# The sixteen routing values of a row block: from the row tile to small tiles loaded five blocks ahead

## The chip, the cores and the metric

The kernel runs on one core of a Trainium2 chip. A core has five engines with instruction queues of their own: TensorE (PE, matmuls), VectorE (DVE), ScalarE (ACT), GpSimd (POOL) and SyncE (SP, here only a DMA queue). The metric is the time of one execution on the device, in microseconds (us); lower is better. A profile of one execution tells what each engine did and what it waited for.

## The reference

Eight sequences of 512 tokens, width 256, float32, go through a state-space layer, a mixture of experts, causal attention and the same mixture again, each with a layer norm ahead and a residual sum. The change lies in the mixture:

```python
combine = (jax.nn.one_hot(topk_idx, E, dtype=tw.dtype) * tw[..., None]).sum(1)
h = jnp.einsum('td,edf->etf', x, gate_w)
u = jnp.einsum('td,edf->etf', x, up_w)
y = jnp.einsum('etf,efd->etd', jax.nn.silu(h) * u, down_w)
routed = jnp.einsum('etd,te->td', y, combine)
```

There are 16 experts with hidden width 256, and each of the 4096 tokens takes its best 4. The kernel computes only these: tokens are sorted by expert, and each expert's tokens are worked on in blocks of 128.

## The kernel before

The kernel has four stages: the scan with the router of the first mixture, the routed experts of the first mixture (`routed(0, ...)`), attention with the router of the second, and the routed experts again (`routed(1, ...)`). The routers write each token's normalised row once for each chosen expert into a DRAM tensor `xg`, sorted by expert. A row of `xg` has 256 values and then 16 routing values: four gains, four expert numbers and eight copies of the token's number.

`routed` works through 136 blocks (a branch for more, `needed > LIKELY`, is not taken with these inputs). For block n:

- `load(n)`, four blocks ahead (`AHEAD`): four DMAs on SP (L874) bring the 256 values of 128 rows, and one DMA on ScalarE (L878) brings the 16 routing values into the same row tile (tag `kb4`, nine buffers). The first two blocks come with one DMA each (L870). The address of a block in `xg` is a register; for every eight blocks `places` loads eight addresses from SBUF on SP and on ScalarE (L848).
- `fetch(n)`: ScalarE and VectorE copy the expert's gate and up weights (L893) into small tiles (tag `col`, six buffers, so three blocks); the expert's place is a register too, loaded for four blocks at a time on TensorE, ScalarE and VectorE (L834).
- `turn(n)`: VectorE transposes the rows (L906).
- `up(n)`: TensorE multiplies (L919, eight matmuls for gate and eight for up as the profile counts them); ScalarE takes the sigmoid (L927); VectorE multiplies twice (L929, L930) and computes each row's gain from the routing values (L934, L942). The PSUM results have two buffers each.
- `down(n)`: TensorE multiplies by the down weights (L949), ScalarE scales by the gain (L957), and GpSimd scatters the rows, adding to a DRAM tensor `parts` (L958), with the token numbers from the routing values as index. Even and odd blocks go to two `parts` tensors.

In program order, iteration n of `run` has `load(n + 4)`, `fetch(n + 1)`, `up(n)`, `turn(n + 2)` and `down(n - 2)`. The framework then orders each engine's instructions by its own plan of times, under dependences; `tc.issue_after(x)` puts an instruction behind x on its engine. Each engine works through its queue in that order. DMAs take completion semaphores in turn, eight for those of SP and ScalarE and eight for GpSimd's, and one is issued only when the last DMA on its semaphore has landed. A tile's buffer is free for a new load when everything that used it is done; for a row tile the scatter is last.

At the start of the kernel, three constants `bp_sb`, `cp_sb` and `bc_all` (L178 to L250) have tiles of their own; `bc_sb` is made from them on VectorE (L198, the line of the helper `by_vector`).

Of the kernel before, what the change touches and what calls it, by code (L numbers as in the profile page):

```python
# [10 lines left out]
FP = mybir.dt.float32  # L11
AF = mybir.ActivationFunctionType
# [19 lines left out]
EG, TKG, TK = 4, 2, 4  # L32
# [3 lines left out]
BLK = P  # L36
# [8 lines left out]
ROW = D + 2 * TK + 8  # L45
# [8 lines left out]
U32 = mybir.dt.uint32  # L54
EPS = 1e-5
CLIP = 10.0
KB, COLS = 9, 6
# [2 lines left out]
SENT = 4  # L60
HELD = 6
AHEAD = 4


SUMMED = {0: DONE[0], 1: 76, 2: 88, 3: 110, 4: 127}
# [12 lines left out]
def tile_hybrid_block(  # L78
# [22 lines left out]
    nc = tc.nc  # L101

    const = ctx.enter_context(tc.tile_pool(name="const", bufs=1))
    xpool = ctx.enter_context(tc.tile_pool(name="xpool", bufs=3))
    work = ctx.enter_context(tc.tile_pool(name="work", bufs=2))
    small = ctx.enter_context(tc.tile_pool(name="small", bufs=2))
# [18 lines left out]
    xg = [dram.tile([NROW, ROW], FP, name=f"xg_{i}") for i in range(2)]  # L125
# [49 lines left out]
    nc.gpsimd.dma_start(out=b_in_sb, in_=b_in.rearrange("(c p) -> p c", p=P))  # L175
    d_sb = const.tile([P, NI], FP, name="d_sb")
    nc.gpsimd.dma_start(out=d_sb, in_=d_skip.rearrange("(c p) -> p c", p=P))
    bp_sb = const.tile([P, NI, DS], FP, name="bp_sb")  # L178
    nc.gpsimd.dma_start(out=bp_sb, in_=b_proj.rearrange("(c p) j -> p c j", p=P))
    cp_sb = const.tile([P, NI, DS], FP, name="cp_sb")  # L180
    nc.gpsimd.dma_start(out=cp_sb, in_=c_proj_t.rearrange("(c p) j -> p c j", p=P))
    w_out_sb = w_scan[:, KD * DI :].rearrange("p (c d) -> p c d", c=NI)
    nc.scalar.dma_start(out=w_out_sb, in_=w_out.rearrange("(c p) d -> p c d", p=P))
# [13 lines left out]
    def by_vector(op, *args):  # L197
        pending.append(lambda: tc.keep_in_program_order(op(*args)))  # L198
# [18 lines left out]
    def load_expert(e: int):  # L217
# [13 lines left out]
        out=before,  # L231
        in_=before,
# [12 lines left out]
    nc.scalar.activation(begun, decay, AF.Sigmoid)  # L245


    bc_all = const.tile([P, NI, DS], FP, name="bc_all")
    by_vector(nc.vector.tensor_mul, bc_all, bp_sb, cp_sb)
    bc_sb = const.tile([P, NI], FP, name="bc_sb")  # L250
    by_vector(nc.vector.tensor_reduce, bc_sb, bc_all, AX.X, ALU.add)
# [1 line left out]
    def load_attention_weights():  # L253
# [16 lines left out]
        out=causal, in_=causal, compare_op=ALU.is_ge, fill=0.0, base=0, pattern=[[0, 2], [1, P]], channel_multiplier=-1  # L270
# [6 lines left out]
        out=tri, in_=tri, compare_op=ALU.is_gt, fill=0.0, base=0, pattern=[[1, P]], channel_multiplier=-1  # L277
# [546 lines left out]
    def routed(i: int, table, beside):  # L824

        weight_at, row_at, expert, many, _ = table
        ACT, DVE = mybir.EngineType.Activation, mybir.EngineType.DVE
        PE, SP = mybir.EngineType.PE, mybir.EngineType.SP
        held, heads, known, turns = {}, set(), set(), {}

        def values(n: int):

            many = min(4, (LIKELY if n < LIKELY else NBLK) - n)
            _, w = nc.values_load_multi_w_load_instructions(  # L834
                weight_at[:, n : n + many],
                engines=[PE, ACT, DVE],
                min_val=0,
                max_val=(E - 1) * WEXP,
                skip_runtime_bounds_check_because="a count of at most E - 1 experts, times WEXP",
            )  # L840
            for j in range(many):
                held[n + j].insert(0, w[j])
                known.add(n + j)

        def places(n: int):

            many = min(8, (LIKELY if n < LIKELY else NBLK) - n)
            _, r = nc.values_load_multi_w_load_instructions(  # L848
                row_at[:, n : n + many],
                engines=[SP, ACT],  # L850
                min_val=0,
                max_val=NROW - BLK,
                skip_runtime_bounds_check_because="the blocks table stays within the sorted rows",
            )
            for j in range(many):
                held[n + j] = [r[j]]

        def load(n: int):
            if n not in held:
                places(n)  # L860
            if n < 2:


                rows = work.tile([P, NT, ROW], FP, tag="rows", name=f"rows_{i}_{n}")
                rows = rows.rearrange("p t c -> p (t c)")[:, 0 : 4 * D]
            else:
                rows = work.tile([P, 4 * D], FP, tag="kb4", name=f"rows_{i}_{n}", bufs=KB)
            block = bass.ds(held[n][-1], BLK)
            if n in heads:
                nc.sync.dma_start(out=rows[:, 0:ROW], in_=xg[i][block, :])  # L870
            else:

                for a in range(QUAD):
                    nc.sync.dma_start(  # L874
                        out=rows[a * SQ : (a + 1) * SQ, 0:D].rearrange("s (b c) -> s b c", b=QUAD),
                        in_=xg[i][block, a * KD * SQ : (a + 1) * KD * SQ].rearrange("(b s) c -> s b c", s=SQ),
                    )
                nc.scalar.dma_start(out=rows[:, D:ROW], in_=xg[i][block, D:ROW])  # L878
            held[n].append(rows)

        def fetch(n: int):
# [29 lines left out]
        def up(n: int):  # L911
            _, _, rows, *both = held[n]


            ph = [bank([P, KF * P], f"ph_{i}_{n}_{s}", f"big{s}") for s in range(2)]
            for s in range(2):
                for f in range(KF):
                    for k in range(KD):
                        nc.tensor.matmul(  # L919
                            ph[s][:, f * P : (f + 1) * P],  # L920
                            lhsT=both[s][:, k * F + f * P : k * F + (f + 1) * P],
                            rhs=rows[:, ROW + k * P : ROW + (k + 1) * P],
                            start=(k == 0),
                            stop=(k == KD - 1),
                        )
            act = rows[:, ROW + D : ROW + D + F]
            nc.scalar.activation(act, ph[0], AF.Sigmoid)  # L927
            with tc.issue_after(turns.pop(n + 1).ins) if n + 1 in turns else nullcontext():
                nc.vector.tensor_mul(act, ph[0], act)  # L929
            made = nc.vector.tensor_mul(act, ph[1], act)  # L930

            gain = small.tile([P, TK + 1], FP, tag="gain", name=f"gain_{i}_{n}", bufs=4)
            with tc.issue_after(made.ins):
                nc.vector.scalar_tensor_tensor(  # L934
                    gain[:, 0:TK],
                    rows[:, D + TK : D + 2 * TK],
                    expert[:, n : n + 1],
                    rows[:, D : D + TK],
                    ALU.is_equal,
                    ALU.mult,  # L940
                )
            nc.vector.tensor_reduce(gain[:, TK : TK + 1], gain[:, 0:TK], AX.X, ALU.add)  # L942
            held[n][3:] = [act, gain]

        def down(n: int):
            w, _, rows, act, gain = held.pop(n)
            py = bank([P, D], f"pyr_{i}_{n}", "y")
            for f in range(KF):
                nc.tensor.matmul(  # L949
                    py,  # L950
                    lhsT=act[:, f * P : (f + 1) * P],
                    rhs=w_all[:, bass.ds(w + 2 * KD * F + f * D, D)],
                    start=(f == 0),
                    stop=(f == KF - 1),
                )

            nc.scalar.mul(rows[:, 0:D], py, gain[:, TK : TK + 1])  # L957
            nc.gpsimd.indirect_dma_start(  # L958
                out=parts[i][n % 2],
                out_offset=bass.IndirectOffsetOnAxis(  # L960
                    ap=rows[:, D + 2 * TK : D + 2 * TK + 1].bitcast(U32), axis=0
                ),
                in_=rows[:, 0:D],
                in_offset=None,
                compute_op=ALU.add,
            )

        def run(first: int, last: int):
            heads.update((first, first + 1))
            coming = iter(range(first, last))  # L970

            def load_to(n: int):
                for m in coming:
                    load(m)
                    if m >= n:
                        break

            load_to(first + AHEAD - 1)
            values(first)
            fetch(first)  # L980
            turn(first)
            for n in range(first, last + 2):
                load_to(n + AHEAD)
                if n + 2 < last and n + 2 not in known:
                    values(n + 2)
                if n + 1 < last:
                    fetch(n + 1)
                if n < last:
# [598 lines left out]
```

## Time and profile before

| | |
|---|---|
| median of three runs | 1736.51 us (1733.36 to 1739.04) |
| profiled execution | 1726.62 us |
| its span, first to last instruction | 1724.9 us |
| mean granted TensorE clock | 0.978 |
| TensorE busy | 1596.2 us (93%) |
| VectorE, ScalarE, GpSimd busy | 1183.2, 717.7, 773.3 us |
| scatters L958 | 272, 1570 ns each on GpSimd |
| address loads L848 on ScalarE | 34, median 1968 ns |
| 16-value loads L878 on ScalarE | 268, median 343 ns to issue |

An engine's busy time is the union of its instructions; DMA issues, register loads and semaphore waits are not counted as busy. A line of the timeline has the start, the duration, the engine (with a q for its sequencer), the source line, the operation, output and inputs, and in brackets how long the engine was idle before and what ended that. [...]

### The profile page before, as it was taken

To read this page: it belongs to the slowest core of one execution; us is meant where nothing else is said; L and a number is where in the kernel's file an instruction comes from. 1 tells how busy PE (TensorE), PEld (TensorE's weight loads), DVE (VectorE), ACT (ScalarE), POOL (GpSimd) and SP (SyncE) were. 2 spreads that over 40 slices of the span, in tenths; PEclk is the share of its full clock that TensorE was granted. 3 is DMA by queue.
4 is the path that set the end of the run, shared out by engine and by line. 5 is a ranking of instruction groups with operands and counts; after the bars stand their busy time and mean duration, and the time that the engine had idled before them with its cause. 6 is when DMAs were issued, how large, how long until landed. Compare 5 with 4: busy or idle time off the path is not lost. (4 is left out here: it accounts for less than half of the span.)

```text
span 1724.9 us, 35522 instructions
## 1 busy us (share of the span) xinstructions
PE 1596.2 (93%) x9912; PEld 1150.6 (67%) x9912; DVE 1183.2 (69%) x3771; ACT 717.7 (42%) x1416; POOL 773.3 (45%) x675
## 2 busy tenths in 40 slices
PE   6899998989999999899999999999899999888884
PEld 3566655589998888854445545544458999888883
DVE  7888877546666666567786686776745866656553
ACT  3223232145554444455544354344214455444441
POOL 3355555535555555430032232232433555555453
PEclk8999999999999999999999999999998999999997
DMA  4454333457776666631012211122545677667667
GB/s 161 143 179 157 136 107 115 161 84 101 101 102 115 93 94 93 100 78 38 25 59 75 70 59 63 58 84 86 183 136 81 98 101 106 115 123 134 104 111 182
DMA packets 297530, 181.63 MB, mean 105 GB/s; under 512 B 204816, under 2 KB 278064, under 8 KB 297328
## 3 DMA queue, kind: packets, MB, share of 16 engines
q0 software_dynamic: 54720, 82.57, 24.9%
q1 hardware_dynamic: 202208, 90.57, 20.6%
q10 hardware_dynamic: 40400, 6.15, 2.1%
q8 instruction: 84, 1.38, 0.3%
q14 instruction: 118, 0.97, 0.2%
HBM read 81.62 MB, written 97.53 MB: 104 GB/s over the span
## 5 line engine op out<-in xcount | busy, mean ns | idle before, releaser
L958 POOL DMA_INDIRECT part<-rows x272 | 427.0, 1570 | 341.2 <-DMA rows<-xg 198.1
L724 POOL DMA_INDIRECT xg<-sorted_m,slots_m x256 | 259.7, 1014 | 322.0 <-ACT slots_m L721 81.6
L919 PE MATMUL ph<-rows,gate 128*128 128x128 f32 x2160 | 291.2, 278 | 43.4 <-DVE rows L906 41.9
L919 PEld LDWEIGHTS ph<-rows,gate 128*128 128x128 f32 x2160 | 279.6, 193 | 75.9 <-issue 44.7
L919 PE MATMUL ph<-rows,up 128*128 128x128 f32 x2160 | 288.1, 277 | 0.0
L949 PE MATMUL pyr<-w_all,rows 128*128 x1088 | 281.9, 383 | 2.9 <-DVE gain L934 2.7
L919 PEld LDWEIGHTS ph<-rows,up 128*128 128x128 f32 x2160 | 265.6, 194 | 0.0
L893 DVE COPY up<-w_all 128x512 f32 x270 | 118.6, 439 | 152.1 <-PE ph L919 125.8
L893 ACT COPY gate<-w_all 128x512 f32 x270 | 166.0, 617 | 125.5 <-PE ph L919 90.9
L949 PEld LDWEIGHTS pyr<-w_all,rows 128*128 128x128 f32 x1088 | 187.7, 193 | 19.3 <-ACT rows L927 3.1
L927 ACT ACTIVATE rows<-ph 128x256 f32<-128x256 f32 x272 | 104.2, 383 | 201.1 <-PE ph L919 169.0
L906 DVE STREAM_TRANSPOSE rows<-rows 128x256 f32<-128x256 f32 x268 | 117.7, 439 | 80.6 <-DMA rows<-xg 72.9
L957 ACT ACTIVATE rows<-pyr,gain 128x256 f32<-128x256 f32 x272 | 128.5, 473 | 87.4 <-PE pyr L949 60.2
L1171 ACT ACTIVATE w_all<-ps_a 128x1024 f32<-128x1024 f32 x128 | 124.4, 1020 | 52.2 <-PE ps_a L1160 47.8
L929 DVE TENSOR_TENSOR rows<-ph,rows 128x256 f32<-128x256 f32 x272 | 106.8, 393 | 46.5 <-ACT rows L927 45.5
L930 DVE TENSOR_TENSOR rows<-ph,rows 128x256 f32<-128x256 f32 x272 | 115.0, 423 | 25.4 <-PE ph L919 1.1
L1160 PE MATMUL ps_a<-w_all 32*128 32x384 f32 (+3 forms) x1024 | 122.2, 475 | 7.7 <-ACT w_all L1171 6.7
L1022 PE MATMUL pg_m<-xT_m,su_sb 128*128 128x512 f32 x256 | 124.8, 609 | 0.0
L1022 PE MATMUL pg_m<-xT_m,sg_sb 128*128 128x512 f32 x256 | 122.4, 600 | 0.0
L1051 PE MATMUL pd_m<-sd_sb,act_m 128*128 128x256 f32 x512 | 121.2, 383 | 0.3 <-DVE act_m L1038 0.2
L1051 PEld LDWEIGHTS pd_m<-sd_sb,act_m 128*128 128x128 f32 x512 | 95.9, 190 | 24.0 <-issue 6.7
L1160 PEld LDWEIGHTS ps_a<-w_all 32*128 32x128 f32 x1024 | 48.4, 186 | 69.4 <-ACT w_all L1171 25.7
(224 smaller groups left out, 1979.7 us busy)
## 6 DMA issues: line engine op xcount, KB each, us to landing
rows<-xg SPq DMA_DIRECT2D x1072, 32.0 KB
part<-x SPq DMA_DIRECT2D x16, 512.0 KB
part<-ys_m SPq DMA_DIRECT2D x14, 512.0 KB
w_all<-in_L_ffn_gate_w_dram SPq DMA_DIRECT2D x24, 256.0 KB
w_all<-in_L_ffn_up_w_dram SPq DMA_DIRECT2D x24, 256.0 KB
w_all<-in_L_ffn_down_w_dram SPq DMA_DIRECT2D x24, 256.0 KB
sum<-part POOLq DMA_DIRECT2D x10, 512.0 KB
xg<-zeros SPq DMA_DIRECT2D x34, 136.0 KB
```

The lines of the kernel that those rows point to most:

```text
L724: nc.gpsimd.indirect_dma_start(out=xg[i], out_offset=bass.IndirectOffsetOnAxis(ap=slots[:, at : at + 1], axis=0), in_=rows[:, t, :], in_of ...
L893: copy(here, w_all[:, bass.ds(held[n][0] + half * KD * F, KD * F)])
L906: turns[n] = nc.vector.transpose(xT.rearrange("p (k b s) -> p k b s", k=KD, b=QUAD), rows[:, 0:D].rearrange("p (b i k) -> p k b i", b=QUAD ...
L919: nc.tensor.matmul(ph[s][:, f * P : (f + 1) * P], lhsT=both[s][:, k * F + f * P : k * F + (f + 1) * P], rhs=rows[:, ROW + k * P : ROW + (k ...
L930: made = nc.vector.tensor_mul(act, ph[1], act)
L949: nc.tensor.matmul(py, lhsT=act[:, f * P : (f + 1) * P], rhs=w_all[:, bass.ds(w + 2 * KD * F + f * D, D)], start=(f == 0), stop=(f == KF - 1),
L957: nc.scalar.mul(rows[:, 0:D], py, gain[:, TK : TK + 1])
L958: nc.gpsimd.indirect_dma_start(out=parts[i][n % 2], out_offset=bass.IndirectOffsetOnAxis(ap=rows[:, D + 2 * TK : D + 2 * TK + 1].bitcast(U ...
L1022: made = nc.tensor.matmul(dst, lhsT=w[:, k, f * P : (f + 1) * P], rhs=xnT[:, k, :], start=(k == 0), stop=(k == KD - 1),)
L1051: nc.tensor.matmul(py[:, j, :], lhsT=acts[n][:, f, t * P : (t + 1) * P], rhs=shared[n][3][:, f, :], start=(n == 0 and f == 0), stop=(n == ...
L1160: nc.tensor.matmul(ps[j // 2][:, j % 2, col : col + n], lhsT=k_sb[w][r, o, c * P : (c + 1) * P], rhs=q_sb[r, o, c * P : T], start=True, st ...
L1171: nc.scalar.activation(es[two], ps[two][:, :, 0:cols], AF.Exp, scale=ATT_SCALE)
```

## The change

The 16 routing values of block n get a small tile `meta` (128 x 16 values, nine buffers, `METAS`) instead of the end of the row tile. A new function `whose(n)` loads it on ScalarE. `run` calls `whose` one block further ahead than `load`: five blocks. In `up(n)` the sigmoid is issued behind the load of block n + 5. The gain and the scatter's index read the small tile. For the first two blocks, whose row comes whole, `metas[n]` is a view of the row tile. The three constants at the start share one tile of the tag `col`, which makes room in SBUF.

```diff
+METAS = 9
...
-    bp_sb = const.tile([P, NI, DS], FP, name="bp_sb")
+    bc_parts = work.tile([P, 3, NI, DS], FP, tag="col", name="bc_parts", bufs=COLS)
+    bp_sb, cp_sb, bc_all = (bc_parts[:, n] for n in range(3))
...
-        def load(n: int):
+        def whose(n: int):
             if n not in held:
                 places(n)
+            if n not in heads:
+                metas[n] = small.tile([P, ROW - D], FP, tag="meta", name=f"meta_{i}_{n}", bufs=METAS)
+                asked[n] = nc.scalar.dma_start(out=metas[n], in_=xg[i][bass.ds(held[n][-1], BLK), D:ROW])
+
+        def load(n: int):
...
-                nc.scalar.dma_start(out=rows[:, D:ROW], in_=xg[i][block, D:ROW])
...
-            nc.scalar.activation(act, ph[0], AF.Sigmoid)
+            with tc.issue_after(asked.pop(n + AHEAD + 1).ins) if n + AHEAD + 1 in asked else nullcontext():
+                nc.scalar.activation(act, ph[0], AF.Sigmoid)
...
-                    rows[:, D + TK : D + 2 * TK],
+                    metas[n][:, TK : 2 * TK],
                     expert[:, n : n + 1],
-                    rows[:, D : D + TK],
+                    metas[n][:, 0:TK],
...
-                    ap=rows[:, D + 2 * TK : D + 2 * TK + 1].bitcast(U32), axis=0
+                    ap=metas.pop(n)[:, 2 * TK : 2 * TK + 1].bitcast(U32), axis=0
...
-            load_to(first + AHEAD - 1)
+            asked.clear()
+            done = {whose: first, load: first}
+
+            def reach(do, n: int):
+                while done[do] < min(n + 1, last):
+                    do(done[do])
+                    done[do] += 1
+
+            reach(whose, first + AHEAD)
+            reach(load, first + AHEAD - 1)
...
-                load_to(n + AHEAD)
+                reach(whose, n + AHEAD + 1)
+                reach(load, n + AHEAD)
```

More of the change, by code (lines that the diff above doesn't have):

```diff
@@ L177, in tile_hybrid_block @@
     nc.gpsimd.dma_start(out=d_sb, in_=d_skip.rearrange("(c p) -> p c", p=P))
-    bp_sb = const.tile([P, NI, DS], FP, name="bp_sb")
+    bc_parts = work.tile([P, 3, NI, DS], FP, tag="col", name="bc_parts", bufs=COLS)
+    bp_sb, cp_sb, bc_all = (bc_parts[:, n] for n in range(3))
     nc.gpsimd.dma_start(out=bp_sb, in_=b_proj.rearrange("(c p) j -> p c j", p=P))
-    cp_sb = const.tile([P, NI, DS], FP, name="cp_sb")
     nc.gpsimd.dma_start(out=cp_sb, in_=c_proj_t.rearrange("(c p) j -> p c j", p=P))
@@ L245, in tile_hybrid_block @@
     nc.scalar.activation(begun, decay, AF.Sigmoid)
-    bc_all = const.tile([P, NI, DS], FP, name="bc_all")
     by_vector(nc.vector.tensor_mul, bc_all, bp_sb, cp_sb)
@@ L828, in routed @@
         PE, SP = mybir.EngineType.PE, mybir.EngineType.SP
-        held, heads, known, turns = {}, set(), set(), {}
+        held, heads, known, turns, metas, asked = {}, set(), set(), {}, {}, {}
         def values(n: int):
@@ L870, in load @@
                 nc.sync.dma_start(out=rows[:, 0:ROW], in_=xg[i][block, :])
+                metas[n] = rows[:, D:ROW]
             else:
@@ L969, in run @@
             heads.update((first, first + 1))
[L970 to L976, printed above, removed]
-            load_to(first + AHEAD - 1)
+            asked.clear()
[6 more added lines that the diff above has]
+            reach(load, first + AHEAD - 1)
             values(first)
```

## The prediction

> **What bounds the kernel now.** I read the page's engine table and slices first, then the routed stages by windows, the waits, and one timeline. The change touches only the two routed expert stages (first to last sigmoid 356.9 to 741.8 us and 1299.7 to 1699.9 us) and one small tile at the start.
>
> ```profile
> span 1724.9 us, 35522 instructions
> PE 1596.2 (93%) x9912; PEld 1150.6 (67%) x9912; DVE 1183.2 (69%) x3771; ACT 717.7 (42%) x1416; POOL 773.3 (45%) x675
> 356.90:550.00 193.10, 190.01 (x1418) 180.00 (x1417) 128.59 (x422) 96.92 (x210) 106.87 (x69) 1.00 0.70 102
> 550.00:741.80 191.80, 176.40 (x1293) 162.28 (x1292) 119.17 (x411) 92.20 (x194) 102.22 (x67) 1.00 0.65 97
> 1299.70:1470.00 170.30, 169.24 (x1257) 160.72 (x1256) 118.27 (x401) 86.34 (x187) 96.16 (x61) 0.99 0.67 98
> 1470.00:1700.00 230.00, 202.73 (x1445) 186.49 (x1444) 134.71 (x439) 102.90 (x217) 121.32 (x86) 0.98 0.69 118
> ```
>
> In the windows the first figure is the length, the second TensorE's busy time. TensorE sets the pace: a block is 16 matmuls L919 (1.78 us in the chain) and 4 L949 (0.87 us), 2.65 us, and 136 blocks are 360 us. In the first half of each stage the sigmoids come 2.73 us apart (blocks 11 to 66). In the second half (66 to 135) they are 2.98 and 3.18 us apart, 23 and 37 us over the matmuls. That loss is what the change could win. The timeline shows its shape, once every eight blocks:
>
> ```profile
> 642.38 0.39 ACT L927 ACTIVATE rows<-ph 128x256 f32<-128x256 f32 x1 [0.42 <-PE ph L919]
> 644.43 0.38 ACTq L878 DMA_DIRECT2D rows<-xg  x1
> 644.97 0.62 ACT L893 COPY gate<-w_all 128x512 f32 x1 [2.21 <-PE pyr L949]
> ...
> 651.34 0.45 DVE L906 STREAM_TRANSPOSE rows<-rows 128x256 f32<-128x256 f32 x1 [2.72 <-DMA rows<-xg]
> ...
> 651.93 1.13 PE L919 MATMUL ph<-rows,gate 128*128 128x128 f32 x8 [2.16 <-DVE rows L906]
> ```
>
> Between 642.38 and 644.43 ScalarE's sequencer loads eight row addresses (L848). The 16-value load of block 104 goes out late, that of 105 at 645.45. Every DMA of SP and ScalarE takes the next of eight completion semaphores and must wait until the last user of that semaphore has landed. In the built program the fourth row DMA of block n follows the 16-value load of the same block in 103 of 134 cases. So SP's rows wait for ScalarE (rows of 105: last DMA 647.81, landed 651.22, by the trace's semaphore times), then the transpose, then TensorE for 2.16 us.
>
> ```profile
> L848 ACTq TENSOR_LOAD <-lines_b x34: 1747/1968/2628, 349.3 to 1670.5; - x34
> SPq L874 <- DMA rows<-xg: 56.3, 36, 4.3
> POOL part L958 <- DMA rows<-xg: 198.1, 145, 15.8
> ```
>
> First the address load (min/median/max ns), then SP's own waits (us, times, longest) in 1400 to 1700 us, then the scatters'. GpSimd's scatter L958 is no idle engine either. By the trace's semaphore times it lands 3.93 us after its start (median), and a scatter to the same `parts` tensor starts 0.72 us after that landing, so two alternating chains need (3.93 + 0.72) / 2 = 2.33 us a block of the 2.65.
>
> [...] L893 above starts only after the DMA issue at 644.43. [...] L848 starts with the sigmoid ahead of it and nothing behind it starts before it ends. [...]
>
> **The change part by part.**
>
> (1) Count. Still 134 loads of 16 values per stage on ScalarE (0.34 us issue each, L878) and 17 address loads. SP keeps 536 row DMAs per stage, its loads of addresses stand one block earlier. The vector ops and scatters read another tile of the same shape. Zero.
>
> (2) Removed: the coupling. A row DMA of block n now follows, on its semaphore, the 16-value load of n+2 or n+3 (in the second half; some n to n+1), whose place is in front of an earlier sigmoid. In the second halves nine groups a stage lie at address loads for blocks 64, 72 ... 128; each costs (2.95 - 2.65) x 8 = 2.4 us now (2.95 is the spacing in stage one, blocks 80 to 135). Gain at most 18 x 2.4 = 43 us.
>
> (3) Added: where the address load falls. Built order on ScalarE at those nine places: gate 103, L848, load 104, sigmoid 99, load 105, sigmoid 100. Gate 103 takes the buffer of gate 100, so sigmoid 99 now stands behind the gate half of block 100. Count from the start of block 99's matmuls: gate half of 100 ends 3.54; gate 103 starts 3.74; L848 starts with it and ends 5.7 (1.97); load 104 and its register steps 0.68 (as at 1468.83 to 1469.51); sigmoid 99 at 6.4, ends 6.8; product L929 0.39, ends 7.2. It frees the PSUM bank of block 101, which TensorE wanted at 4.43: 2.9 us idle. Down 99 comes a block later than usual (built order of TensorE: 100, 101, down 99), so scatter 99 lands late for load 108, which sigmoid 103 is queued behind: another 0.6 us. 3.5 x 18 = +63 us. Behind sigmoid 99 are all of that ScalarE queue: gates, scalings (so scatters), sigmoids.
>
> (4) Added: the wait for the scatter. With nine small tiles, load m waits for the landing of scatter m-9. Before, the same wait (through the rows tile) named a scatter six or seven blocks behind the next sigmoid; no sigmoid came within 0.3 us of it. After, the load stands five or, by the scheduler, six blocks ahead, so the scatter is only four or three blocks behind. Laid over this trace:
>
> ```profile
> 456.24 1.55 POOL L958 DMA_INDIRECT part<-rows  x1 [0.65 <-ACT gate L893]
> 458.91 0.38 ACT L927 ACTIVATE rows<-ph 128x256 f32<-128x256 f32 x1
> ```
>
> This is scatter 35 and sigmoid 38 of stage one; the built program puts load 44 (waits for scatter 35) in front of sigmoid 38. Scatter 35 landed at 460.37, plus 0.5 for the issue: sigmoid 38 would be 2.0 us late. In blocks 11 to 66, 29 and 26 sigmoids of the two stages wait for a scatter three back, 2.7 us late on average; those four back are about even. The product of a sigmoid has 1.1 us before its down matmul is due (L930 ends 1403.13 + about 0.2, L949 at 1404.40). Going block by block, adding to a running delay what exceeds 1.1 us and moving later scatters by it, blocks 11 to 66 give 25 and 20 us: +45. Bounds: if the scatters started 0.27 us after scaling as the best do, three blocks of 7.95 us just hold the loop (scaling 0.72, 0.27, landing 3.93, issue 0.5, sigmoid to product 1.37, 0.2, down 0.87 = 7.86) and it costs 0; if gates and scalings queued behind the waits are counted too, working blocks 38 to 43 by hand gives 4.3 us in five blocks, 95 us for 110.
>
> (5) Start: `bc_parts` takes one of six `col` buffers till L198 at 25.6 us, and the third scan (1.22 us, then at 21.1) moves behind it: 0 to 2 us, I take 0.
>
> Sum: -43 + 63 + 45 = +65 us. On the profiled execution's 1726.6 us (span 1724.9 and 1.7 around it): 1792. The median of the runs is 9.9 us higher; same difference, 1736.5 + 65 = 1801.
>
> **Rivals.** (A) The decoupling wins and sigmoids' delays are hidden: waits in (3) and (4) fall in slack of TensorE, (2) remains: 1736.5 - 43 = 1694; half hidden gives about 1715. For it: ScalarE is busy only 42%. Against: both waits sit on an in-order engine, and TensorE has a PSUM bank pair of two blocks only. It decides if a scatter starts under 0.3 us after its scaling nearly always; the mean is 1.2 and 1.9 us. (B) Loss and gain cancel: (4) is small because a slower rhythm empties the scatters' queue, (3) costs its 2.9 alone: -43 + 52 + 10 = +19, about 1755; the lower end of this is 1740. (C) ScalarE's order becomes the bound: gates and scalings held behind the loads delay scatters again, +95 for (4): 1736.5 + 115 = 1851 and above. (D) The change does not do what it says: the loads could have stayed near their old place. The built order excludes it: 127 of 134 are six or seven blocks past the last sigmoid ahead of them.
>
> **How the numbers follow.** The measurement tells 0.3% (5 us) from no change. Main case, 1765 to 1840: 0.62. C, above 1840: 0.14. B, 1740 to 1765: 0.11, of which 0.03 lies within 5 us of before. A: 0.13, of which 0.02 is no change. So faster 0.11, same 0.05, slower 0.84. The range from 1740 to 1862 leaves out A and the top of C.
>
> **What would show it.** Right: ScalarE idle in front of L927's successor (sigmoid) grows and its releaser is a scatter (`part<-rows`) or a load on ScalarE's queue; TensorE waits for the product L929 or the sigmoid, no longer for the transpose; the spacing in blocks 11 to 66 rises from 2.73 to about 3.1 us and in the groups of eight from 23.6 to about 24.7; SP's waits for DMA fall. Step (3) is wrong if TensorE stays busy at those nine places, step (4) if the sigmoids of blocks 11 to 66 keep their time. A median under 1731 makes the prediction wrong: then the waits did not reach TensorE.

## The result, and the profile after

The kernel after takes 1938.04 us (median of four runs, 1931.64 to 1943.46), the kernel before, timed beside it, 1734.93 us. The ratio is 1.117 (95% interval 1.112 to 1.122): 203 us slower, where the prediction said 65.

The page of the kernel after, its first lines and two of its groups (busy us, mean ns, and the idle time ahead with what ended it), and then the same two groups of the kernel before:

```profile
span 1936.4 us, 35528 instructions
PE 1676.4 (87%) x9912; PEld 1201.0 (62%) x9912; DVE 1198.5 (62%) x3771; ACT 698.2 (36%) x1416; POOL 774.1 (40%) x675
...
L935 DVE TENSOR_TENSOR rows<-ph,rows 128x256 f32<-128x256 f32 x272 | 113.3, 416 | 306.2 <-ACT rows L933 304.5
L933 ACT ACTIVATE rows<-ph 128x256 f32<-128x256 f32 x272 | 103.7, 382 | 319.2 <-DMA part<-rows,meta 116.2 <-PE ph L924 77.9 <-DMA meta<-xg 45.6
```

```profile
L929 DVE TENSOR_TENSOR rows<-ph,rows 128x256 f32<-128x256 f32 x272 | 106.8, 393 | 46.5 <-ACT rows L927 45.5 <-ACT gate L893 0.8
L927 ACT ACTIVATE rows<-ph 128x256 f32<-128x256 f32 x272 | 104.2, 383 | 201.1 <-PE ph L919 169.0 <-DMA rows<-xg 14.4 <-PE pyr L949 13.4
```

ScalarE is less busy than before (36% against 42%) and still it holds the others up: VectorE's product L935 waits 304.5 us for the sigmoid L933 (before 45.5 us, L929), and the sigmoid waits 116.2 us for a scatter (`part<-rows,meta`), for which it never waited before. The two routed stages in halves, columns as in the prediction:

```profile
361.90:600.00 238.10, 198.77 (x1345) 178.61 (x1344) 125.51 (x401) 87.41 (x200) 100.26 (x65) 0.95 0.54 77
600.00:844.40 244.40, 203.54 (x1356) 186.68 (x1354) 131.08 (x432) 91.67 (x203) 106.97 (x70) 0.92 0.56 81
1417.10:1660.00 242.90, 202.31 (x1371) 181.33 (x1371) 133.46 (x440) 89.86 (x204) 102.80 (x67) 0.96 0.55 79
1660.00:1908.90 248.90, 201.03 (x1318) 185.77 (x1318) 126.03 (x399) 88.36 (x197) 112.04 (x79) 0.92 0.58 97
```

From first to last sigmoid the two stages took 785 us and now take 974 us, 189 of the 211 us between the two spans. Not only the second halves: the sigmoids of blocks 11 to 66 stood 2.73 and 2.74 us apart and now stand 3.65 and 3.63. From block 66 to 135 it was 2.98 and 3.18 and is 3.60 and 3.78.

The waits of the kernel after (us, times, longest), ScalarE's and then SP's, the last with SP's line of before under it:

```profile
ACT rows L933 <- DMA part<-rows,meta: 116.2, 58, 4.6
...
ACT gate L898 <- DMA part<-rows,meta: 52.5, 24, 4.3
...
ACT rows L963 <- DMA part<-rows,meta: 30.7, 11, 4.1
```

```profile
SPq L880 <- DMA meta<-xg: 329.0, 140, 6.8
SPq L874 <- DMA rows<-xg: 119.7, 87, 4.3
```

The same scatter holds sigmoids, gate copies and scalings, for all three stand behind a load on ScalarE. In both traces ScalarE's 1416 instructions start in the order of the built program, and none starts before a DMA issue (277) or an address load (34) ahead of it has ended. SP's row loads wait 329 us for 16-value loads; before they waited 119.7 us for loads into the row tiles. The tie between the two queues was to be loosened, and SP waits more. Little of that reaches TensorE: the transposes wait 41.7 us for rows where they waited 72.9, and TensorE waits 36.6 us for transposes where it waited 41.9.

The timeline shows the wait for the scatter, first on ScalarE, then GpSimd's scatters, in the first stage:

```profile
512.46 0.34 ACTq L863 DMA_DIRECT2D meta<-xg  x1
512.85 0.38 ACT L933 ACTIVATE rows<-ph 128x256 f32<-128x256 f32 x1 [3.48 <-PE ph L924]
514.36 0.34 ACTq L863 DMA_DIRECT2D meta<-xg  x1
514.87 0.62 ACT L898 COPY gate<-w_all 128x512 f32 x1 [1.64 <-DMA part<-rows,meta]
515.39 0.38 ACT L933 ACTIVATE rows<-ph 128x256 f32<-128x256 f32 x1
515.67 0.61 ACT L898 COPY gate<-w_all 128x512 f32 x1
516.17 0.84 ACT L963 ACTIVATE rows<-pyr,gain 128x256 f32<-128x256 f32 x2
```

```profile
508.48 1.56 POOL L964 DMA_INDIRECT part<-rows,meta  x1 [3.70 <-ACT rows L933]
510.35 1.55 POOL L964 DMA_INDIRECT part<-rows,meta  x1 [0.30 <-issue]
516.92 1.55 POOL L964 DMA_INDIRECT part<-rows,meta  x1 [5.03 <-DMA rows<-xg]
```

The scatter at 508.48 is that of block 40. By the trace's semaphore times it landed at 512.44, and 0.02 us later load 49 went out, with sigmoid 43 behind it (the bracket names TensorE, which had long been done). Scatter 41 landed at 514.34; load 50 went out at 514.36, and behind it stood a gate copy, sigmoid 44, another gate copy and only then, at 516.17, the scalings of blocks 42 and 43. So scatter 42 starts at 516.92 and scatter 43, on the other `parts` tensor, at 518.78, 10.3 us after scatter 40: a closed round of three blocks. Laid over the whole trace, 183 of 246 loads (load m, for blocks 13 to 135 of both stages) go out within 0.15 us of the landing of scatter m-9. In the kernel before there is none.

The built order differs in a second way. TensorE's down matmuls of a block usually stand behind the gate and up matmuls of the next block. In the kernel after, those of 95 of the 272 blocks stand behind one block more ("a block later" below); in the kernel before those of 18.

### The profile page after: what moved, and what is told of

It reads as the page before. It is cut to its first block, busy times and chain, and to the rows that moved or that the text cites. A ratio compares the mean times of both kernels' runs of the same rounds, so it can differ in the third digit from the quotient of the medians.

```text
span 1936.4 us, 35528 instructions
## 1 busy us (share of the span) xinstructions
PE 1676.4 (87%) x9912; PEld 1201.0 (62%) x9912; DVE 1198.5 (62%) x3771; ACT 698.2 (36%) x1416; POOL 774.1 (40%) x675
## 5 line engine op out<-in xcount | busy, mean ns | idle before, releaser
L964 POOL DMA_INDIRECT part<-rows,meta x268 | 420.4, 1569 | 524.1 <-ACT rows L963 172.1
L924 PE MATMUL ph<-rows,gate 128*128 128x128 f32 x2160 | 316.7, 293 | 108.2 <-DVE rows L935 65.2
L924 PEld LDWEIGHTS ph<-rows,gate 128*128 128x128 f32 x2160 | 296.0, 205 | 151.2 <-issue 105.5
L955 PE MATMUL pyr<-w_all,rows 128*128 x1088 | 296.1, 397 | 57.6 <-DVE gain L940 47.7
L924 PE MATMUL ph<-rows,up 128*128 128x128 f32 x2160 | 308.2, 290 | 0.0
L935 DVE TENSOR_TENSOR rows<-ph,rows 128x256 f32<-128x256 f32 x272 | 113.3, 416 | 306.2 <-ACT rows L933 304.5
L924 PEld LDWEIGHTS ph<-rows,up 128*128 128x128 f32 x2160 | 286.7, 207 | 0.0
L955 PEld LDWEIGHTS pyr<-w_all,rows 128*128 128x128 f32 x1088 | 194.8, 200 | 87.9 <-ACT rows L963 35.6
L933 ACT ACTIVATE rows<-ph 128x256 f32<-128x256 f32 x272 | 103.7, 382 | 319.2 <-DMA part<-rows,meta 116.2
L911 DVE STREAM_TRANSPOSE rows<-rows 128x256 f32<-128x256 f32 x268 | 117.5, 438 | 47.7 <-DMA rows<-xg 41.7
L936 DVE TENSOR_TENSOR rows<-ph,rows 128x256 f32<-128x256 f32 x272 | 114.1, 420 | 31.4 <-PE ph L924 12.4
```

The lines of the kernel that those rows point to most:

```text
L911: turns[n] = nc.vector.transpose(xT.rearrange("p (k b s) -> p k b s", k=KD, b=QUAD), rows[:, 0:D].rearrange("p (b i k) -> p k b i", b=QUAD ...
L924: nc.tensor.matmul(ph[s][:, f * P : (f + 1) * P], lhsT=both[s][:, k * F + f * P : k * F + (f + 1) * P], rhs=rows[:, ROW + k * P : ROW + (k ...
L955: nc.tensor.matmul(py, lhsT=act[:, f * P : (f + 1) * P], rhs=w_all[:, bass.ds(w + 2 * KD * F + f * D, D)], start=(f == 0), stop=(f == KF - 1),
L964: nc.gpsimd.indirect_dma_start(out=parts[i][n % 2], out_offset=bass.IndirectOffsetOnAxis(ap=metas.pop(n)[:, 2 * TK : 2 * TK + 1].bitcast(U ...
```

## The experiments

The theory: the cost is this closed round (scatter, load, sigmoid, product, down, scaling, scatter), closed by the place of the load and by its nine tiles, with the address load L848 in front of a sigmoid on top. The rivals: the address load is nearly all of it; any load tied to the front of a sigmoid costs by itself; the start part. "Ahead" counts blocks from the next sigmoid behind a load to the load's own block; "back" counts from that sigmoid's block to the block whose scatter frees the tile. With nine tiles, five ahead is four back, and six ahead three back. The kernel before was timed again beside every group of experiments, and its median moved between 1730.9 and 1762.3 us, so ratios to it are compared. A share of 0.01 is 17 us.

**The scatter's wait taken away.** Twelve tiles of 12 values instead of nine of 16, and every load held behind the sigmoid six blocks back. This holds the loads five blocks ahead, so it also moves most of those that were six ahead; the next experiment makes that move alone:

```diff
-METAS = 9
+METAS = 12
...
-                metas[n] = small.tile([P, ROW - D], FP, tag="meta", name=f"meta_{i}_{n}", bufs=METAS)
-                asked[n] = nc.scalar.dma_start(out=metas[n], in_=xg[i][bass.ds(held[n][-1], BLK), D:ROW])
+                metas[n] = small.tile([P, 12], FP, tag="meta", name=f"meta_{i}_{n}", bufs=METAS)
+                with tc.issue_after(sigs[n - 6].ins) if n - 6 in sigs else nullcontext():
+                    asked[n] = nc.scalar.dma_start(out=metas[n], in_=xg[i][bass.ds(held[n][-1], BLK), D : D + 12])
...
-                nc.scalar.activation(act, ph[0], AF.Sigmoid)
+                sigs[n] = nc.scalar.activation(act, ph[0], AF.Sigmoid)
```

> The kernel after with twelve small tiles instead of nine (each 12 values wide, the 9 that are used and three more, so that twelve fit), and every load held between the sigmoids of the sixth and the fifth block ahead, so that ScalarE's order stays what it was and the load now waits for the scatter seven blocks back from the next sigmoid instead of four or three. Theory (the loop): the cost is the round scatter, load, sigmoid, product, down, scaling, scatter; with three more blocks of room it falls out, the sigmoids of blocks 11 to 66 return from 3.6 to 2.7 or 2.8 us apart and the time to 1740 to 1800 us (what is left is the address load in front of a sigmoid, at most 63 us by the prediction, less up to 43 us gained). Rival 1 (address load L848 in front of the sigmoid): nothing but the groups of eight counts, the time stays above 1880 us. Rival 2 (any load ahead of a sigmoid holds ScalarE, whatever it waits for): above 1880 us too, with the sigmoid's idle time still put down to a DMA.

Measured: 1788.66 us, ratio 1.034 (1.031 to 1.037). Blocks 11 to 66 stand 2.84 and 2.79 us apart. One of 246 loads goes out with the landing of its scatter. The sigmoid's group, and SP's waits:

```profile
L934 ACT ACTIVATE rows<-ph 128x256 f32<-128x256 f32 x272 | 104.4, 384 | 177.6 <-PE ph L925 125.5 <-issue 42.6 <-DMA meta<-xg 9.3
```

```profile
SPq L881 <- DMA meta<-xg: 162.9, 110, 5.5
```

The scatter is gone from the sigmoid's waits, and TensorE, which should be the one it waits for, is back in first place. Between 1.117 and 1.034 lie 145 us: the wait for the scatter is the larger part of the loss, and a load in front of a sigmoid is not slow by itself. The rivals fall as main causes, but 3.4% is left.

**Four blocks back for all.** Nine tiles, and every load exactly five blocks ahead (in the kernel after of the 278 loads in the built order, the branch not taken among them, 178 are five and 80 are six blocks ahead of the next sigmoid):

```diff
-                asked[n] = nc.scalar.dma_start(out=metas[n], in_=xg[i][bass.ds(held[n][-1], BLK), D:ROW])
+                with tc.issue_after(sigs[n - 6].ins) if n - 6 in sigs else nullcontext():
+                    asked[n] = nc.scalar.dma_start(out=metas[n], in_=xg[i][bass.ds(held[n][-1], BLK), D:ROW])
```

> The kernel after with nine tiles, only that every load is held behind the sigmoid six blocks back, so that all stand five blocks ahead and none six: the scatter waited for is four blocks back from the next sigmoid for all of them, where in the kernel after about a third were three back. Theory (the loop): the period is the round divided by the number of blocks in it; a round of about 10.9 us (three blocks of 3.63 us) over four blocks is 2.7 us, so the time falls clearly, to 1760 to 1860 us. If the loop is a mix that the four-back loads bound as well, 1860 to 1920. Rivals (address load, order alone): 1920 to 1945 us, no change.

Measured: 1891.00 us, ratio 1.094 (1.090 to 1.098); blocks 11 to 66 at 3.35 and 3.42 us; 179 of 246 loads go out with the landing. One block more of room for a third of the loads gives back 40 us, but a scatter four blocks back binds too: between this kernel and the one with twelve tiles, whose loads stand at the same distance, lie the other 104 of the 145 us. The clean division of a fixed round by the number of blocks, 2.7 us, is wrong: four blocks of 3.35 to 3.42 us are 13.4 to 13.7 us, so the round got longer with its room.

**The old distance.** Small tiles, loads three blocks ahead, the scatter six back:

```diff
-                asked[n] = nc.scalar.dma_start(out=metas[n], in_=xg[i][bass.ds(held[n][-1], BLK), D:ROW])
+                with tc.issue_after(sigs[n - 4].ins) if n - 4 in sigs else nullcontext():
+                    asked[n] = nc.scalar.dma_start(out=metas[n], in_=xg[i][bass.ds(spot[n], BLK), D:ROW])
...
-            with tc.issue_after(asked.pop(n + AHEAD + 1).ins) if n + AHEAD + 1 in asked else nullcontext():
+            with tc.issue_after(asked.pop(n + 3).ins) if n + 3 in asked else nullcontext():
...
-                reach(whose, n + AHEAD + 1)
+                reach(whose, n + 3)
```

(`spot` keeps the address register, since the row load may now come first.)

> Nine small tiles and the start part kept, but each load stands three blocks ahead, between the sigmoids of the fourth and the third block before its own, as in the kernel before, so the scatter it waits for is six back. Theory (the loop, set off by the place of the load): within 30 us of the kernel before, 1700 to 1765 us, and if the tie between SP's row loads and ScalarE's loads is really gone, up to 40 us below it. Rival 2 (a load tied to the front of a sigmoid costs by itself): above 1850 us. Rival 1 (address load in front of the sigmoid): it now stands in front of the row loads of a block four ahead, 1760 to 1800 us.

Measured: 1749.71 us, ratio 1.011 (1.007 to 1.014). Of the 203 us, 185 are gone. The small tiles and the tie to the sigmoid are still there; what changed is the place of the loads and, with it, the rest of the built order: the address load now goes with the row load, and the down matmuls of only 18 blocks stand a block later, as in the kernel before. So this run takes away the wait for the scatter and moves the address loads together.

**The tile alone.** The kernel before with nine small tiles and the start part, loaded in `load` after the row DMAs, with no tie and not five ahead:

```diff
-                nc.scalar.dma_start(out=rows[:, D:ROW], in_=xg[i][block, D:ROW])
+                metas[n] = small.tile([P, ROW - D], FP, tag="meta", name=f"meta_{i}_{n}", bufs=METAS)
+                nc.scalar.dma_start(out=metas[n], in_=xg[i][block, D:ROW])
```

> The kernel before with the small tiles alone: nine of them and the start part, but each load is written where it was, behind the block's row loads four blocks ahead, and nothing ties it to a sigmoid. The order that is built from it puts most loads five or six blocks ahead of the next sigmoid all the same, because the small tile comes free before anything else does. Theory (the loop through the scatter that frees the tile, set off by the place of the load and not by the tie): clearly slow, 1830 to 1950 us. Rival (the tie to the sigmoid or the program's five blocks ahead is the cost): 1715 to 1765 us.

Measured: 1900.45 us, ratio 1.087 (1.081 to 1.094).

```profile
L929 ACT ACTIVATE rows<-ph 128x256 f32<-128x256 f32 x272 | 104.0, 383 | 241.2 <-DMA part<-rows,meta 102.0 <-PE ph L921 97.7 <-issue 24.1
```

The sigmoid waits for the scatter here too, though the source writes each load four blocks ahead: in the built order 159 of 278 loads stand five or six blocks ahead of the next sigmoid, as the expectation says because the small tile comes free first. The line `issue_after` is not needed for the loss; a tile of its own is enough. Nor are the later down matmuls, of which this kernel has only 24.

**Addresses four at a time**, in the kernel after, in the twelve-tile kernel and in the kernel before:

```diff
-            many = min(8, (LIKELY if n < LIKELY else NBLK) - n)
+            many = min(4, (LIKELY if n < LIKELY else NBLK) - n)
```

> The kernel after with four row addresses loaded at a time instead of eight, twice as many address loads of (by the four-value load of the weights, 0.31 us) a sixth of the length. Theory (the loop): only step (3) of the prediction can go, at most 63 us, and less where the loop covers it: 1870 to 1935 us. Rival 1 (the address load is the cost): below 1800 us.

> The twelve-tile kernel (each load five blocks ahead, waiting for the scatter seven blocks back from the next sigmoid) with four row addresses loaded at a time instead of eight. With eight it stood at 1788.7 us, its second halves at 3.29 and 3.33 us a block against 2.98 and 3.18 in the kernel before. Theory (what is left there is step (3) of the prediction, the eight-address load of 1.97 us in front of a sigmoid): the second halves fall to 2.75 to 3.0 us and the time to 1735 to 1765 us. Rival (what is left is the length of the queue on ScalarE or the twelve tiles themselves): 1775 to 1795 us, no change.

> The kernel before with four row addresses loaded at a time instead of eight. Step (2) of the prediction puts 43 us of the kernel before on the late load behind the eight-address load of 1.97 us. If that is right: 1690 to 1720 us. If the second halves' 23 and 37 us come from something else (the row loads' wait for ScalarE as such, or the scatters): 1725 to 1735 us, no change. Slower by 10 us or more would say that two short address loads cost more than a long one.

Measured: 1.113 (1.107 to 1.119) where the kernel after has 1.117; 1.049 (1.044 to 1.053) where twelve tiles with eight addresses have 1.034; 1.008 (1.005 to 1.010) for the kernel before. No gain in the first beyond the measurement, and a loss in the other two: the second run went against its theory and its rival both, and the third, 14 us slower, is what its expectation named as the sign that two short loads cost more than a long one. The second is no clean test: with four addresses the down matmuls of 145 blocks stand a block later, with eight those of 100. The address load of four in the third of these:

```profile
L848 ACTq TENSOR_LOAD <-lines_b x68: 907/919/1264, 364.6 to 1719.2; - x68
```

Half as many addresses take half as long, 0.92 us instead of 1.97, twice as often (1.10 us in the twelve-tile kernel): here the time is by the address. The expectation had taken 0.31 us from the load of four weights (L834), and that was wrong. This says nothing yet against step (3).

**Loads by SP.** The kernel before with the 16-value loads and all addresses on SP:

```diff
-                nc.scalar.dma_start(out=rows[:, D:ROW], in_=xg[i][block, D:ROW])
+                nc.sync.dma_start(out=rows[:, D:ROW], in_=xg[i][block, D:ROW])
...
-                engines=[SP, ACT],
+                engines=[SP],
```

> The kernel before with the 16-value loads issued by SP behind the four row loads of their block, and the row addresses loaded on SP alone: ScalarE has neither loads nor address loads in the routed stages. If ScalarE's part in the order of transfers is what cost 43 us (step (2)): 1685 to 1715 us. If SP's own queue (a fifth issue per block, its own address loads of 1.72 us) is what counts: 1725 to 1760 us. The loop of the kernel after can't arise, since SP's queue holds no sigmoid.

Measured: 1790.42 us, ratio 1.021 (1.018 to 1.024), worse than either theory had it. Blocks 11 to 66 stand 3.14 and 3.03 us apart, and VectorE's transpose waits 133.7 us for rows (before 72.9). The rows come later in this kernel, in which SP issues the fifth transfer as well. How much of that is issue and how much waiting was not separated.

**ScalarE's address loads taken away.** Only the first eight addresses of a stage are loaded on ScalarE and used again for all later blocks, in the twelve-tile kernel and in the kernel before. The routing values are then those of one of the first eight blocks, so the scatters go to other rows (one holds GpSimd for 1567 ns with the address loads and without). In the twelve-tile kernel the built order changes too: the down matmuls of 19 blocks stand a block later, not of 100.

```diff
-                engines=[SP, ACT],
+                engines=[SP] if n - min(ring, default=n) >= 8 else [SP, ACT],
...
-                    asked[n] = nc.scalar.dma_start(out=metas[n], in_=xg[i][bass.ds(held[n][-1], BLK), D : D + 12])
+                    asked[n] = nc.scalar.dma_start(out=metas[n], in_=xg[i][bass.ds(ring[min(ring) + (n - min(ring)) % 8], BLK), D : D + 12])
```

> The twelve-tile kernel (1.034 of the kernel before) without ScalarE's address loads: only the first eight-address load of each stage stays, and all later 16-value loads take those eight addresses again and again, so every later block works with the routing values of one of the first eight blocks (that part of the computation is changed; SP's row loads, the weights, and the number and kind of all transfers stay). Theory (step (3) of the prediction: the 1.97 us of the address load in front of a sigmoid is what is left): second halves from 3.29 and 3.33 us a block to 2.9 or less, ratio to the kernel before 0.99 to 1.01. Rival (what is left is the small tiles' transfers and the place of the loads, not the address load): ratio 1.025 to 1.04.

> The kernel before with the same part changed: ScalarE loads row addresses only once a stage, and all later 16-value loads take the first eight addresses again. Theory (step (2): the address load on ScalarE holds back the load of 16 values and through it SP's rows, 43 us): ratio 0.970 to 0.985. If SP's own address load (1.72 us, the same eight-block rhythm) is what holds the rows: ratio 0.995 to 1.005.

Measured: 0.998 (0.995 to 1.000) for twelve tiles, from 1.034: 63 us. The second halves fall from 226.8 and 230.0 us to 194.2 and 204.5. In the kernel before 0.988 (0.983 to 0.992): 22 us, between what the two theories expected, so the address loads of ScalarE in the kernel before cost half of what step (2) said.

Where these 63 us arise, the waits of TensorE show, first with twelve tiles and the address loads in place, then in the kernel after (neither the kernel before nor the twelve-tile kernel without address loads has such a line):

```profile
PE ph L925 <- DVE rows L936: 63.7, 17, 4.6
PE ph L924 <- DVE rows L935: 65.2, 17, 4.6
```

TensorE waits for the product behind a late sigmoid. In the second halves of the twelve-tile kernel 15 of these waits make 57 of the 60 us in which it stands idle for more than 0.15 us at a time, and each ends within 8 us of the start of an address load.

**The start part alone**, in the kernel before:

```diff
-    bp_sb = const.tile([P, NI, DS], FP, name="bp_sb")
+    bc_parts = work.tile([P, 3, NI, DS], FP, tag="col", name="bc_parts", bufs=COLS)
+    bp_sb, cp_sb, bc_all = (bc_parts[:, n] for n in range(3))
```

> The kernel before with the start part alone: the two projections and their product in one of the six large column buffers. The first sigmoid of the routed stage came at 361.9 us in the kernel after and at 356.9 in the kernel before. If the start part does that: ratio 1.002 to 1.004 and a first sigmoid 3 to 5 us later. If it is of no account, as step (5) took it: ratio 0.998 to 1.002.

Measured: 1.002 (0.999 to 1.004). No effect shown; at most 7 us.

**Addresses shifted by four bytes.** The table has two rows of 143 four-byte values: weights from byte 0, addresses from byte 572, which is 12 past a multiple of 16. One spare column puts them at 576, and the built order stays as it is:

```diff
-        lines = work.tile([1, 2, NBLK], I32, tag="col", name=f"lines_{tag}", bufs=COLS)
+        lines = work.tile([1, 2, NBLK + 1], I32, tag="col", name=f"lines_{tag}", bufs=COLS)
...
-        table += [lines[:, 0, :], lines[:, 1, :], expert, many, nb]
+        table += [lines[:, 0, 0:NBLK], lines[:, 1, 0:NBLK], expert, many, nb]
```

(The two writes to the table take `0:NBLK` as well.) It ran on the kernel before, on the twelve-tile kernel, on the kernel after and on the kernel with late loads:

> The kernel before with the table of weights and addresses made 144 columns wide instead of 143, so that the addresses begin at byte 576 instead of 572. Theory (a load of several values is slow because its first value does not lie on a multiple of 16 bytes: 0.24 us for each of eight addresses, 0.31 us for four weights together): the address load falls from 1.97 to 0.3 to 0.6 us on ScalarE and from 1.72 to the same on SP, and the time by up to the 22 us that leaving it out gave, ratio 0.985 to 0.995. Rival (addresses cost more by their kind): address load and time unchanged, ratio 0.998 to 1.002.

> The twelve-tile kernel with the addresses shifted the same way. Theory: with an address load of 0.3 to 0.6 us step (3) shrinks from 63 us to 10 or 20 us, ratio to the kernel before 1.000 to 1.012 instead of 1.034. Rival (the place of the address load costs, whatever its length, or it does not get shorter): ratio 1.025 or more.

> The kernel after with the addresses shifted the same way. Theory (the loop through the scatter bounds it, the address load comes on top): a part of the 63 us is gained, ratio 1.08 to 1.105 instead of 1.117. If the loop hides the address load whole: 1.11 to 1.12. Rival (the address load is the main cost): below 1.05.

> The kernel with small tiles whose loads stand three blocks ahead (1.011 of the kernel before), with the addresses shifted. Theory: the scatter is far enough back and the address load short, so what the change removes, SP's rows waiting for ScalarE's late load, is gone without a price: ratio 0.98 to 0.995, level with or a little below the kernel before with the shift alone. Rival (small tiles cost something by themselves): ratio 1.00 to 1.01.

The address loads of the kernel before so shifted, on SP and on ScalarE, and under them SP's before the shift (min/median/max ns; ScalarE's is in the prediction):

```profile
L848 SPq TENSOR_LOAD <-lines_b x34: 363/527/1182, 357.0 to 1673.5; - x34
L848 ACTq TENSOR_LOAD <-lines_b x34: 535/548/886, 366.1 to 1676.3; - x34
L848 SPq TENSOR_LOAD <-lines_b x34: 1662/1720/2546, 336.3 to 1667.4; - x34
```

The same eight addresses take 0.55 us on ScalarE instead of 1.97, and 0.53 on SP instead of 1.72. Times:

| | eight addresses | shifted |
|---|---|---|
| kernel before | 1 | 0.987 (0.982 to 0.992) |
| small tiles, loads three ahead | 1.011 (1.007 to 1.014) | 0.993 (0.990 to 0.996) |
| twelve tiles, loads five ahead | 1.034 (1.031 to 1.037) | 1.008 (1.005 to 1.010) |
| kernel after | 1.117 (1.112 to 1.122) | 1.099 (1.093 to 1.104) |

The kernel before with the shift alone is faster than both kernels, 1737.81 us against 1762.31 beside it, and gains as much as leaving the address loads out (0.988). The waits of its transposes for rows, and under them those of the kernel before:

```profile
DVE rows L906 <- DMA rows<-xg: 48.8, 50, 3.8
DVE rows L906 <- DMA rows<-xg: 72.9, 54, 5.3
```

With both repairs, late loads and the shift, the change is within the range that its theory gave, but not level with the shift alone: 1749.77 us against 1737.81 in runs side by side, a loss of 12 us or 0.6 to 0.7%. So the change brings no gain even so, and the small tiles seem to cost a little by themselves; why was not taken apart.

## Why the prediction was wrong

The sign was right and the size was not: +203 us against +65, above the range. By the ratios the 203 us are made up so (each is a difference of two measured ratios times 1735, so the sum comes out by construction):

| | predicted | measured | from |
|---|---|---|---|
| (2) address load of the kernel before, gone | -43 | -22 | 1 to 0.988 |
| (3) address load in front of a sigmoid, with later down matmuls | +63 | +63 | 0.998 to 1.034 |
| (4) wait for scatter m-9 | +45 | +145 | 1.034 to 1.117 |
| (5) start, and the rest of the change | 0 | +17 | 0.988 to 0.998 |

**Step (4) failed**: it priced the wait for the scatter at 45 us, and 145 were measured. Four of its terms were too small.

- It counted only blocks 11 to 66. There the kernel after loses 90 us against the twelve-tile kernel (55 blocks times 0.81 and 0.83 us); in the second halves it loses 52 more (248.3 - 226.8 and 260.9 - 230.0), which the sum did not have at all.
- It took the sigmoids whose scatter is four blocks back as "about even". With all loads four back the kernel is still at 1.094, 104 us over the one with twelve tiles.
- It let a late load delay only the sigmoid and took the scalings and gates behind it as on time. ScalarE's queue holds them as well: 52.5 us of waits on gates, 30.7 on scalings.
- It laid the new waits over the trace of before, and so took the round at its old length. From the start of a sigmoid to the end of its block's scaling the median was 5.2 and 5.3 us before and is 6.9 and 7.3 after. Not all of this comes from the wait: with twelve tiles, where the scatter does not bind, it is already 6.4, with about as many down matmuls a block later (100, after 95, before 18). The step noted such a later place only beside the address loads.

The time from sigmoid to scaled rows is inside the round, so a delay in it comes back three or four blocks later. The step had named this case as its upper bound, 95 us for blocks 11 to 66, worked out by hand over five blocks; 90 was measured there. That the upper value was the one to take, because a closed round repeats a delay and does not absorb it, is argued from the timeline above and from the spacing, not measured apart. Its lower bound of 7.86 us for three blocks used the shortest time of every link, 3.2 us from sigmoid to scaled rows, where the trace of before already had 5.2.

**Step (3)** had the right place and about the right size: with address loads the twelve-tile kernel is 58 us longer in the second halves, 3.2 us at each of the 18 groups of eight, against 3.5 predicted (of which its own figures give 2.8 us idle rather than 2.9). That both totals are 63 us is in part luck. The measured step holds the later down matmuls too. Shortening the address loads from 1.97 to 0.55 us at an unchanged order (and SP's as well) gave 0.026 with twelve tiles, 45 us; how the other 17 us divide between the remaining length and the order is open. In the kernel after TensorE stands idle for the product as long as with twelve tiles (65.2 and 63.7 us). The shift gave 0.018 there, 32 us, but the intervals do not tell this from 0.026.

**Step (2)** saw the loss in the kernel before rightly at the address loads, but took the whole excess over the matmuls, 43 us, where 22 were to be had, and expected SP's rows to be freed. They were tied again, since the 16-value loads that they follow now waited for scatters: 329 us of waits where the prediction said that they would fall. What gives the 22 us back is a shorter address load (0.987), not the other tile.

**Step (1)**, no instruction more, holds; **step (5)**, nothing at the start, agrees with 1.002 (0.999 to 1.004). The 17 us of the last line of the table are what the small tiles and the early loads cost without scatter and without ScalarE's address loads, where the sum had nothing; their cause stays open.

**The rivals.** What came is (C), with the mechanism it named, gates and scalings held behind the loads, at a chance of 0.14. Its +95 us for the scatter was 50 too low, so the time lies 87 us over the 1851 from which it counted up. (A) and (B) are out. (D), that the loads do not move, is out. Of the signs named, the sigmoid's wait for `part<-rows`, TensorE's wait for the product (65.2 us for L935, the address loads' sign) and the wider spacing of blocks 11 to 66 came, the last with 3.65 us instead of 3.1. The fall of SP's waits did not, and TensorE's waits for the transpose, which were to vanish, only went from 41.9 to 36.6 us.

## What to carry to other kernels

Before a load is moved ahead on an engine that also computes, find what frees its buffer, and count how many blocks back that stands from the next instruction behind the load: if the freeing work depends on that engine, it is a closed round. Price it with everything queued behind the wait and for every block, not as a one-time delay, and on the round of the new built order, not of the old trace. A tile of its own is not neutral: here it let the scheduler move most loads one or two blocks further ahead than the source had them. And where a register load on a sequencer is long, look at the address of its first value before you look at its place: here eight values took 1.97 us from byte 572 and 0.55 us from byte 576.

## What the runs showed of the hardware that was not expected

The time of a register load from SBUF depended on where its values lie, counted in bytes from the start of the table. Beginning 12 bytes past a multiple of 16, eight values took 1.97 us on ScalarE and four took 0.92 us (1.10 in the twelve-tile kernel); beginning on a multiple of 16, eight took 0.55 us and four 0.31 (L834). One value, of another tile, took 0.29 us (L1000). That is 0.23 to 0.27 us a value at the first place and 0.07 to 0.08 at the second, for eight values a factor of 3.6. The cause was not taken apart, no other place was tried, and so whether a multiple of 8 would do in place of 16 is open.

TensorE's own time grew with its idle time. In the two stages it was busy 738 us before and 806 after with the same matmuls, and the granted clock of the whole execution fell from 0.978 to 0.946. So of the 189 us in the two stages, 122 are idle time of TensorE and 67 longer busy time. With twelve tiles it was busy for 755 us at a clock of 0.963, in the kernel before with shifted addresses for 730 us at 0.971. Which of the two follows the other was not tested; with the scatter's wait taken away, 51 of the 67 us and 0.017 of the 0.032 of clock came back.
